# Ternary weights prepared in 42 pieces, one order of halves in the fp4 stages, memories prepared in the first attention

## The chip, the cores and the metric

The kernel runs on one core of one Trainium2 chip. The metric is device time in microseconds (us); lower is better. It runs one fixed program over a batch of 8 sequences of 1024 tokens with 256 features, in float32.

## The reference, cut to what matters

Six sublayers follow each other, each on a layer norm of x:

```python
x = x + 0.5 * fp4_ffn(layernorm(x))        # blockwise FP4 rounding of inputs, weights and hidden values
x = x + decay_attention(layernorm(x))      # a decaying state per head
x = x + 0.5 * fp4_ffn(layernorm(x))
x = x + 0.5 * ternary_ffn(layernorm(x))    # W1, W2 rounded to -1, 0, 1; gelu between them
x = x + memory_attention(layernorm(x))     # linear attention beside 4 stored memories
x = x + 0.5 * ternary_ffn(layernorm(x))
```

The ternary rounding takes one scale for a whole matrix, so nothing can be rounded before everything has been summed:

```python
scale = max(mean(abs(w)), 1e-8)
w_t = clip(round(w / scale), -1, 1)
```

The FP4 rounding scales each block of 16 values by its largest magnitude and rounds to eight magnitudes.

## The kernel before, in words

The 8192 tokens are 64 tiles of 128 rows; four tiles are a group (G = 4), so there are 16 groups. x stays in SBUF through all six stages. The stages run one after the other: `ffn_fp4`, `attn_decay`, `ffn_fp4`, `ffn_ternary`, `attn_memory`, `ffn_ternary`.

The order of instructions on each engine is written out by hand: `pin` ties an instruction behind the last pinned one on its engine, so each engine works its list strictly in order. A late instruction therefore holds everything behind it on the same engine.

**An fp4 stage** is a loop over iterations i, one tile each (i is its number, j = i % 4 its place in the group). In iteration i:
- PE multiplies x of the tile with gate and up weights (pg, pu at L835), turns the scales of tile i-1 (pts, L863), and multiplies tile i-4 with the down weights (po, L932).
- ACT does silu (sg, L846), copies scales (L790), takes magnitudes of tile i-1 (qp, L795) and copies the turned scales (sct, L869).
- VectorE (DVE) forms h = sg * pu (L848), rounds h of tile i-1 to the grid in two steps (L858), finds the scales of h (L783 to L787), and adds po to x at the end of the iteration (L941).
- POOL multiplies h by the inverse scales (h, L791) and the turned grid by its scales (ht, L899), which for tile i-3 comes in iteration i.
- SP issues the DMAs: scales out (sd, L871), the transpose of the grid (gt, L884), the spread scales back (L876).

**The coming group's input** goes the same way, half a group (two tiles, 512 columns) at a time: normalise on ACT (xn, L317 and L325, four instructions a half), scale on DVE (xn, L783) and POOL (xn, L791), magnitudes on ACT (mgx) and grid on DVE (L858), transpose by DMA (gtx, L1048), multiply on POOL (xt, L899). xn is one buffer. For group t the first half is normalised in iteration 4t-7 and the second in 4t-5 (odd iterations), scaled in 4t-6 and 4t-4, rounded in 4t-5 and 4t-3. The transposed grid lies in xn itself, so a half of xn is written again only when its transpose has been read.

**Layer norm statistics** are planned ahead: `statistics(sizes, dues)` spreads the shares (one per tile, four sets of terms per batch of groups; L235 to L264) evenly over the iterations before each batch is due. `PLANS` holds the sizes and due iterations. What is due at 0 is done in the last iterations of the stage before (`begin`).

**Side work of the first fp4 stage** hangs at the end of each iteration, in `prepared(i)`, behind that iteration's L941:
- the FP4 rounding of the down weights (iterations 1 to 5),
- the decay tables for the attention (`prep_decay`, POOL, iterations 7, 11, 15, 19),
- the ternary weights. Each matrix is 2048 columns of 128 partitions. Its load is issued in iteration 7 (w1) and 27 (w2); then come, in every fourth iteration, the sums (one reduction over 2048, L683), the total (a matmul and two small instructions), and two halves of rounding of 1024 columns, each of three DVE instructions (L699, L700, L703). That is 4 pieces a matrix, in iterations 11, 15, 19, 23 and 31, 35, 39, 43.
- in iteration 44 `prep_memory`: one DMA (b2h), 16 POOL and 3 DVE instructions (L720 to L741) that make tables for the later stages.

**The first attention** (`attn_decay`) is a loop over the same 64 tiles; DVE weighs scores (L1259), POOL only adds a bias to x once a group.

Of the kernel before, what the change touches and what calls it, by code (L numbers as in the profile page):

```python
# [18 lines left out]
P = 128  # L19
# [20 lines left out]
def macaron_kernel(  # L40
# [227 lines left out]
    def statistics(sizes, dues):  # L268
# [75 lines left out]

    NT = NG * G
    PLANS = {
        "start": ((2, 1, 1, 2, 4, 4, 2), [max(0, G * (g - 2) + 1) for g in range(NG)]),
        "fp4": ((2, 1, 1, 2, 4, 4, 2), [max(0, G * (g - 2) + 1) for g in range(NG)]),

        "decay": ((2, 2, 4, 4, 4), [max(0, G * g - 5) for g in range(NG)]),  # L350
        "ternary": ((2, 2, 4, 4, 4), [max(0, g - 1) for g in range(NG)]),
# [321 lines left out]

    def prep_ternary(w, raw_w, prep, ps, tag):

        n0 = w.shape[1]
        n = n0 * w.shape[2]
        ab = prep.tile([P, 1], F32, tag="t_ab", name="t_ab")
        rc = prep.tile([P, 1], F32, tag="t_rc", name="t_rc")

        def sums():
            pin(
                nc.vector.tensor_reduce(  # L683
                    ab, raw_w.rearrange("p k n -> p (k n)"), AX.X, ALU.add,
                    apply_absolute_value=True,
                )
            )

        def total():
            pa = ps.tile([P, 1], F32, tag=tag, name="pa")  # L690
            pin(nc.tensor.matmul(pa, lhsT=ones, rhs=ab, start=True, stop=True))
            pin(nc.vector.tensor_scalar(rc, pa, 1.0 / (P * n), 1e-8, ALU.mult, ALU.max))
            pin(nc.vector.reciprocal(rc, rc))

        def rounded(q):
            part = slice(q * n0 // 2, (q + 1) * n0 // 2)
            wf = raw_w[:, part, :].rearrange("p k n -> p (k n)")
            lo = prep.tile([P, n // 2], F32, tag="t_lo", name="t_lo")
            pin(nc.vector.tensor_scalar(wf, wf, rc, None, ALU.mult))  # L699
            pin(nc.vector.tensor_scalar(lo, wf, -0.5, None, ALU.is_lt))  # L700

            pin(
                nc.vector.scalar_tensor_tensor(  # L703
                    w[:, part, :].rearrange("p k n -> p (k n)"), wf, 0.5, lo,
                    ALU.is_gt, ALU.subtract,
                )
            )

        return sums, total, lambda: rounded(0), lambda: rounded(1)

    memb = w_l1.tile([P, 2, NM, 2, HD], F32, name="memb")

# [32 lines left out]
    def ffn_fp4(prepare, after):  # L745
        with ExitStack() as st:
# [150 lines left out]
            def multiplied(wide, grid):  # L897
                pin(
                    nc.gpsimd.tensor_tensor(  # L899
                        wide.rearrange("p c t -> p (c t)"), grid.rearrange("p c t -> p (c t)"),  # L900
                        wide.rearrange("p c t -> p (c t)"), ALU.mult,
                    )
                )
# [42 lines left out]
            def prepared(i):  # L946

                if i in (1, 3):
                    prep_down_scale(i // 2)
                elif i in (2, 4):  # L950
                    prep_down(i // 2 - 1)
                if i == DOWN:
                    raw_stack.close()
                    load_a0()
                if i % G == 3 and i < 5 * G and i > G:
                    prep_decay(i // G - 1)
                for k, i0 in enumerate((7, 27)):
# [27 lines left out]
            sc1 = fp4_scale(v1, lnp, nc.gpsimd, pin)  # L985
            xts[1] = (xn1,)

            xn = None
            downs = 0

            def x_part(half):
                return xn[:, 2 * half : 2 * half + 2, :].rearrange("p t d -> p (t d)")

            for i in range(NT + 3):
                g, j = divmod(i, G)
                h = hp.tile([P, NI], F32, tag="h", name="h") if i < NT else None

                to = (i + 7) // G
                to_do = to < NG and i > 0
                half = 0 if j in (1, 2, 3) else 1  # L1000
                if i == 0 and not prepare:
                    xts[0], copied = turn_products(xts[0])
                    copied()
# [37 lines left out]
                        round_(part, sc, mg, nc.vector if q else nc.gpsimd)  # L1041
                if pts is not None:
                    spread(i - 1, pts)
                for to_, half_ in list(xgrids):
# [5 lines left out]
                if i == 0:  # L1050
                    mgs = [qp[:, 0 : 2 * D], ps_t.tile([P, 2 * D], F32, tag="pt", name="mg1")]
                    for n in range(2):
# [1 line left out]
                if 0 < i < NT:  # L1054

                    ln.advance(i - 1, 1)
                if to_do and j % 2 == 1:
                    if j == 1:
                        to_n, tiles = to, (0, 1)
                        if xn is None:  # L1060
                            xn = xn_pool.tile([P, G, D], F32, tag="xn", name="xn")
                    else:
                        to_n, tiles = (i + 5) // G, (2, 3)
                    if to_n < NG:
                        for n in tiles:
                            ln.normalize(xn, to_n, n, pin)
                if by_dma(i - 3):
                    scaled_turn(i - 3)
                if NT - 2 <= i - 2 < NT:
                    turn(i - 2)  # L1070
                for key in list(xgrids):
                    gt, at = xgrids[key]
                    if at == i - 2:
                        xgrids.pop(key)
                        to_m, half_m = key
                        multiplied(xts[to_m][:, G * half_m : G * half_m + G, :], gt)
                if i < NT:
                    own = scales[i % 2] if by_dma(i) else None
                    if own is not None:
                        scale(h, hp, NI, sc=own[:, : NI // 16])  # L1080
                        hs[i] = (h, own)
                    else:
                        hs[i] = (h, scale(h, hp, NI) if i < NT - 1 else None)

                    if j % 2 == 0 and i > 1:
                        to_s, half_s = ((i + 6) // G, 0) if j == 2 else ((i + 4) // G, 1)
                        if 1 < to_s < NG:
                            scale(
                                x_part(half_s), lnp, NI + 88,
                                sc=own[:, NC * 8 : NC * 8 + 2 * D // 16],  # L1090
                            )
                            xhalf[i] = (to_s, half_s)
                    if j % 2 == 1 and i > 1:
                        to_r, half_r = ((i + 5) // G, 0) if j == 3 else ((i + 3) // G, 1)
                        if 1 < to_r < NG:
                            v = x_part(half_r)
                            mg = ps_t.tile([P, 2 * D], F32, tag="pt", name="mgx")
                            magnitudes(v, mg)
                            gx = v.bitcast(BF16)[:, 0 : 2 * D]
                            round_grid(v, mg, gx)  # L1100
                            xgrids[to_r, half_r] = (gx, i)
# [252 lines left out]
    def attn_decay(after):  # L1354
        with ExitStack() as st:
# [101 lines left out]
            for i in range(n + 3):  # L1457
# [627 lines left out]
```

## Time and profile before

| | us |
|---|---|
| median of 3 runs | 2608.78 (2608.46 to 2609.09) |
| profiled execution | 2604.35 |
| its span (first to last instruction) | 2602.6 |
| PE busy | 2504.2 (96%) |
| DVE busy | 2107.9 (81%) |
| ACT busy | 1235.8 (47%) |
| POOL busy | 902.6 (35%) |

The stages, by the lines that stand in the trace: the first fp4 stage begins its tiles at 37 us and ends near 540, the first attention runs to about 1000, the second fp4 stage to about 1490, and the two ternary stages with the second attention between them fill the rest.

How to read it: "busy" is time in which an engine executed instructions, registers and waits not counted. Idle time of an engine that is not the bottleneck costs nothing, so a share over the whole span says little about one stage. Where a stage is measured in what follows, it is cut out of the span in us from the first instruction. A tile of an fp4 stage is counted from the first sg<-pg (L846) of one tile to that of the next. DVE and POOL durations are those of single instructions; a duration longer than the instruction's usual one means that it was held while it ran.

### The profile page before, as it was taken

To read this page: it belongs to the slowest core of one execution; us is meant where nothing else is said; L and a number is where in the kernel's file an instruction comes from. 1 tells how busy PE (TensorE), PEld (TensorE's weight loads), DVE (VectorE), ACT (ScalarE), POOL (GpSimd) and SP (SyncE) were. 2 spreads that over 40 slices of the span, in tenths; PEclk is the share of its full clock that TensorE was granted. 3 is DMA by queue.
4 is the path that set the end of the run, shared out by engine and by line. 5 is a ranking of instruction groups with operands and counts; after the bars stand their busy time and mean duration, and the time that the engine had idled before them with its cause. 6 is when DMAs were issued, how large, how long until landed. Compare 5 with 4: busy or idle time off the path is not lost.

```text
span 2602.6 us, 52695 instructions
## 1 busy us (share of the span) xinstructions
PE 2504.2 (96%) x20426; PEld 1864.2 (72%) x20426; DVE 2107.9 (81%) x5040; ACT 1235.8 (47%) x2785; POOL 902.6 (35%) x895
## 2 busy tenths in 40 slices
PE   4899999999999998999999999999999999999999
PEld 2566776766666665677777789995677767678998
DVE  7899999858777678998889789657888888879864
ACT  5344444433433333444444366665555555437664
POOL 4555555521100102555555400004555555540000
PEclk9899999999999999999999999999999999999999
DMA  7455565510000001556555300000000000000001
GB/s 218 99 111 120 119 114 112 110 32 2 2 2 2 2 2 29 113 117 116 115 114 118 81 1 1 1 1 1 2 2 2 2 2 2 2 2 25 33 33 42
DMA packets 197883, 130.32 MB, mean 50 GB/s; under 512 B 137824, under 2 KB 173696, under 8 KB 197632
## 3 DMA queue, kind: packets, MB, share of 16 engines
q1 hardware_dynamic: 196688, 125.75, 22.3%
q8 instruction: 161, 2.64, 0.4%
q0 software_dynamic: 240, 0.54, 0.1%
q14 instruction: 90, 0.74, 0.1%
q10 hardware_dynamic: 704, 0.66, 0.1%
HBM read 78.67 MB, written 16.52 MB: 37 GB/s over the span
## 4 chain that ended last, share of the span: by engine, by line
PE 80%; DVE 11%; ACT 3%; DMA 3%; issue 2%; POOL 1%; SPq 1%; DVEq 0%; POOLq 0%; ACTq 0%
PE po L932 10%; PE po L1207 9%; PE pg L835 9%; PE ph L1180 9%; PE pu L835 8%; PE sc L1250 5%; PE py L1334 5%; PE pq L1348 4%; PE pkv L1348 4%; PE pk L1348 4%; PE po L1348 4%; PE py L1316 2%; PE pmo L1765 2%; DVE at L1259 1%; DMA gtx<-xn 1%
## 5 line engine op out<-in xcount | busy, mean ns | idle before, releaser
L835 PE MATMUL pg<-wgu,xt 128*128 128x352 f32 x1024 | 350.0, 465 | 13.4 <-ACT sg L846 13.1
L932 PE MATMUL po<-wd,ht 128*128 128x256 f32 x1536 | 356.0, 382 | 2.3 <-DVE x L941 1.8
L835 PE MATMUL pu<-wgu,xt 128*128 128x352 f32 x1024 | 348.9, 464 | 2.1 <-DVE h L848 1.9
L932 PEld LDWEIGHTS po<-wd,ht 128*128 128x128 f32 x1536 | 291.7, 191 | 66.0 <-issue 4.1
L791 POOL TENSOR_TENSOR h<-h,q_rs 128x704 f32<-128x704 f32 (+1 forms) x128 | 176.3, 1378 | 419.9 <-DVE q_rs L787 419.9
L846 ACT ACTIVATE sg<-pg 128x352 f32<-128x352 f32 x256 | 117.8, 460 | 399.3 <-PE pg L835 394.0
L835 PEld LDWEIGHTS pg<-wgu,xt 128*128 128x128 f32 x1024 | 194.9, 192 | 108.5 <-ACT sg L846 21.1
L835 PEld LDWEIGHTS pu<-wgu,xt 128*128 128x128 f32 x1024 | 187.1, 193 | 103.3 <-issue 14.7
L1207 PE MATMUL po<-w,hl 128*128 128x256 f32 x1024 | 243.9, 280 | 1.4 <-DVE hl L1191 1.2
L1207 PE MATMUL po<-w,hh 128*128 128x256 f32 x1024 | 243.4, 280 | 0.0
L1881 POOL TENSOR_TENSOR mo<-mo 128x256 f32<-128x256 f32 x192 | 164.3, 856 | 195.0 <-DVE mo L1778 186.5
L899 POOL TENSOR_TENSOR ht<-gt,ht 128x768 f32<-128x768 bf16 x124 | 206.4, 1664 | 0.0
L1180 PE MATMUL ph<-xh,w 128*128 128x512 f32 x512 | 204.4, 401 | 1.4 <-ACT hf L1188 0.6
L1180 PE MATMUL ph<-xl,w 128*128 128x512 f32 x512 | 202.2, 396 | 0.0
L1191 DVE TENSOR_TENSOR hl<-hf,hh 128x512 fp32r<-128x512 f32 x256 | 168.2, 683 | 39.6 <-ACT hh L1189 36.1
L1207 PEld LDWEIGHTS po<-w,hl 128*128 128x128 f32 x1024 | 192.1, 188 | 4.5 <-DVE hl L1191 2.5
L1207 PEld LDWEIGHTS po<-w,hh 128*128 128x128 f32 x1024 | 192.0, 188 | 2.6 <-DVE x L1215 0.3
L848 DVE TENSOR_TENSOR h<-sg,pu 128x352 f32<-128x352 f32 x256 | 131.6, 514 | 60.0 <-PE pu L835 53.1
L1188 ACT ACTIVATE hf<-ph,b1c 128x512 f32<-128x512 f32 x256 | 168.3, 696 | 18.5 <-PE ph L1180 16.1
L1259 DVE TENSOR_TENSOR at<-sc,dec 128x512 f32<-128x512 f32 x256 | 158.5, 681 | 16.6 <-PE sc L1250 16.5
L1259 DVE TENSOR_TENSOR at<-sc,tri 128x512 f32<-128x512 f32 x256 | 164.6, 678 | 0.4 <-PE sc L1250 0.4
L1189 ACT CAST hh<-hf 128x512 fp32r<-128x512 f32 x256 | 149.2, 628 | 17.0 <-PE po L1207 15.2
(276 smaller groups left out, 5304.0 us busy)
## 6 DMA issues: line engine op xcount, KB each, us to landing
ht<-sd SPq DMA_DIRECT2D x124, 384.0 KB
xt<-sd SPq DMA_DIRECT2D x56, 256.0 KB
sd<-sct SPq DMA_DIRECT2D x124, 64.0 KB
x<-in_x SPq DMA_DIRECT2D x15, 512.0 KB
out<-x SPq DMA_DIRECT2D x15, 512.0 KB
raw_w<-in_w_t SPq DMA_DIRECT2D x2, 1024.0 KB
gt<-gd SPq DMA_TRANSPOSE x124
gtx<-xn SPq DMA_TRANSPOSE x56
```

The source lines that it names most:

```text
L791: pin(mul.tensor_tensor(vb, vb, rs[:, :, None].to_broadcast([P, nb, 16]), ALU.mult))
L835: nc.tensor.matmul(ps, lhsT=xts[g][:, 2 * j + k, :], rhs=wgu[:, k, (2 * q + of_up) * NHALF : (2 * q + of_up + 1) * NHALF], start=(k == 0), ...
L899: nc.gpsimd.tensor_tensor(wide.rearrange("p c t -> p (c t)"), grid.rearrange("p c t -> p (c t)"), wide.rearrange("p c t -> p (c t)"), ALU. ...
L932: nc.tensor.matmul(po, lhsT=ht[:kn, c, :], rhs=wd[:kn, c, :], start=(c == 0), stop=(c == NC - 1),)
L1180: nc.tensor.matmul(ph, lhsT=w1[:, k, f * P : (f + 1) * P], rhs=xt[:, k, :], start=(k == 0 and xt is xh), stop=(k == 1 and xt is xl),)
L1188: nc.scalar.activation(hf, ph, AF.Gelu, bias=b1c[:, f : f + 1])
L1189: nc.scalar.copy(hh[:, f, :], hf)
L1191: nc.vector.tensor_tensor(hl[:, f, :], hf, hh[:, f, :].bitcast(F32), ALU.subtract)
L1207: nc.tensor.matmul(po, lhsT=ht[:, f, j * P : (j + 1) * P], rhs=w2[:, f, :], start=(f == 0 and ht is hh), stop=(f == NF - 1 and ht is hl),)
L1259: nc.vector.tensor_tensor(at, sc.rearrange("p m (e t) -> p (m e) t", e=2), weight, ALU.mult)
L1348: nc.tensor.matmul(dst, lhsT=lhsT, rhs=rhs, start=n == 0, stop=n == len(parts) - 1)
L1881: summed = nc.gpsimd.tensor_tensor(mo[:, :, :, 0, :], mo[:, :, :, 0, :], mo[:, :, :, m, :], ALU.add)
```

## The change

- `PLANS`: in the stage that follows the start, each batch of statistics is due one iteration later (4g-6 in place of 4g-7); in "fp4" (the second fp4 stage) the first batch has three groups in place of two, all done ahead of the stage.
- Halves: for every group from the third on both halves follow one table. The first half is normalised and scaled in iteration 4t-6 and rounded in 4t-5; the second in 4t-4 and 4t-3. Scaling and rounding stay in their iterations; normalising moves one iteration later, into the one that scales. The gtx transpose and POOL's xt multiplication swap places in the text of an iteration.
- Ternary weights: the sums come in four parts of 512 columns, the rounding in 16 parts of 128, one piece in every iteration: 21 pieces a matrix, 42 in all. w1: sums in iterations 9 to 12, total in 13, rounding in 14 to 29. w2 is loaded in 34: sums in 36 to 39, total in 40, rounding in 41 to 56. The three instructions of a rounding piece are the same as before.
- `prep_memory` moves from iteration 44 of the first fp4 stage to iteration 24 of the first attention.

```diff
-        "start": ((2, 1, 1, 2, 4, 4, 2), [max(0, G * (g - 2) + 1) for g in range(NG)]),
-        "fp4": ((2, 1, 1, 2, 4, 4, 2), [max(0, G * (g - 2) + 1) for g in range(NG)]),
+        "start": (
+            (2, 1, 1, 2, 4, 4, 2), [0 if g < 2 else G * (g - 2) + 2 for g in range(NG)]
+        ),
+        "fp4": ((3, 1, 2, 4, 4, 2), [0 if g < 3 else G * (g - 2) + 2 for g in range(NG)]),
...
-        def sums():
+        n_sums, n_parts = 4, 16
+        def sums(q):
+            part = slice(q * n // n_sums, (q + 1) * n // n_sums)
...
         def total():
-            pa = ps.tile([P, 1], F32, tag=tag, name="pa")
+            pa = ps.tile([P, n_sums], F32, tag=tag, name="pa")
             pin(nc.tensor.matmul(pa, lhsT=ones, rhs=ab, start=True, stop=True))
-            pin(nc.vector.tensor_scalar(rc, pa, 1.0 / (P * n), 1e-8, ALU.mult, ALU.max))
+            pin(nc.vector.tensor_reduce(rc, pa, AX.X, ALU.add))
+            pin(nc.vector.tensor_scalar(rc, rc, 1.0 / (P * n), 1e-8, ALU.mult, ALU.max))
             pin(nc.vector.reciprocal(rc, rc))
         def rounded(q):
-            part = slice(q * n0 // 2, (q + 1) * n0 // 2)
-            lo = prep.tile([P, n // 2], F32, tag="t_lo", name="t_lo")
+            part = slice(q * n // n_parts, (q + 1) * n // n_parts)
+            lo = prep.tile([P, n // n_parts], F32, tag="t_lo", name="t_lo")
             pin(nc.vector.tensor_scalar(wf, wf, rc, None, ALU.mult))
             pin(nc.vector.tensor_scalar(lo, wf, -0.5, None, ALU.is_lt))
...
-                for k, i0 in enumerate((7, 27)):
+                for k, i0 in enumerate((7, 34)):
...
-                    if i0 < i <= i0 + 16 and i % G == i0 % G:
-                        raw_w[1][(i - i0) // G - 1]()
-                    if i == i0 + 16:
+                    if i0 + 1 < i <= i0 + 1 + 21:
+                        raw_w[1][i - i0 - 2]()
+                    if i == i0 + 22:
                         raw_w_stack.close()
-                if i == 44:
-                    with behind():
-                        prep_memory()
...
+            norms, x_scales, x_rounds = {}, {}, {}
+            for t in range(2, NG):
+                for half in range(2):
+                    at = G * t - 6 + 2 * half
+                    norms[at] = x_scales[at] = x_rounds[at + 1] = (t, half)
...
-                if to_do and j % 2 == 1:
-                    if j == 1:
-                        to_n, tiles = to, (0, 1)
...
+                if i in norms:
+                    if xn is None:
+                        xn = xn_pool.tile([P, G, D], F32, tag="xn", name="xn")
+                    t, half = norms[i]
+                    for n in (2 * half, 2 * half + 1):
+                        ln.normalize(xn, t, n, pin)
...
+                if i == 24:
+                    with behind():
+                        prep_memory()
```

More of the change, by code (lines that the diff above doesn't have):

```diff
@@ L674, in prep_ternary @@
     def prep_ternary(w, raw_w, prep, ps, tag):
-        n0 = w.shape[1]
-        n = n0 * w.shape[2]
-        ab = prep.tile([P, 1], F32, tag="t_ab", name="t_ab")
+        wv = w.rearrange("p k n -> p (k n)")
+        rv = raw_w.rearrange("p k n -> p (k n)")
+        n = rv.shape[1]
+        n_sums, n_parts = 4, 16
+        ab = prep.tile([P, n_sums], F32, tag="t_ab", name="t_ab")
         rc = prep.tile([P, 1], F32, tag="t_rc", name="t_rc")
-        def sums():
+        def sums(q):
+            part = slice(q * n // n_sums, (q + 1) * n // n_sums)
             pin(
                 nc.vector.tensor_reduce(
-                    ab, raw_w.rearrange("p k n -> p (k n)"), AX.X, ALU.add,
-                    apply_absolute_value=True,
+                    ab[:, q : q + 1], rv[:, part], AX.X, ALU.add, apply_absolute_value=True
                 )
@@ L689, in total @@
         def total():
-            pa = ps.tile([P, 1], F32, tag=tag, name="pa")
+            pa = ps.tile([P, n_sums], F32, tag=tag, name="pa")
             pin(nc.tensor.matmul(pa, lhsT=ones, rhs=ab, start=True, stop=True))
-            pin(nc.vector.tensor_scalar(rc, pa, 1.0 / (P * n), 1e-8, ALU.mult, ALU.max))
+            pin(nc.vector.tensor_reduce(rc, pa, AX.X, ALU.add))
+            pin(nc.vector.tensor_scalar(rc, rc, 1.0 / (P * n), 1e-8, ALU.mult, ALU.max))
             pin(nc.vector.reciprocal(rc, rc))
         def rounded(q):
-            part = slice(q * n0 // 2, (q + 1) * n0 // 2)
-            wf = raw_w[:, part, :].rearrange("p k n -> p (k n)")
-            lo = prep.tile([P, n // 2], F32, tag="t_lo", name="t_lo")
+            part = slice(q * n // n_parts, (q + 1) * n // n_parts)
+            wf = rv[:, part]
+            lo = prep.tile([P, n // n_parts], F32, tag="t_lo", name="t_lo")
             pin(nc.vector.tensor_scalar(wf, wf, rc, None, ALU.mult))
@@ L703, in rounded @@
                 nc.vector.scalar_tensor_tensor(
-                    w[:, part, :].rearrange("p k n -> p (k n)"), wf, 0.5, lo,
-                    ALU.is_gt, ALU.subtract,
-                )
-            )
-        return sums, total, lambda: rounded(0), lambda: rounded(1)
+                    wv[:, part], wf, 0.5, lo, ALU.is_gt, ALU.subtract
+                )
+            )
+        return (
+            [lambda q=q: sums(q) for q in range(n_sums)] + [total]
+            + [lambda q=q: rounded(q) for q in range(n_parts)]
+        )
     memb = w_l1.tile([P, 2, NM, 2, HD], F32, name="memb")
@@ L996, in ffn_fp4 @@
                 h = hp.tile([P, NI], F32, tag="h", name="h") if i < NT else None
-                to = (i + 7) // G
-                to_do = to < NG and i > 0
-                half = 0 if j in (1, 2, 3) else 1
                 if i == 0 and not prepare:
@@ L1043, in ffn_fp4 @@
                     spread(i - 1, pts)
+                if i == 0:
+                    mgs = [qp[:, 0 : 2 * D], ps_t.tile([P, 2 * D], F32, tag="pt", name="mg1")]
+                    for n in range(2):
+                        magnitudes(v1[:, 2 * D * n : 2 * D * (n + 1)], mgs[n])
+                if 0 < i < NT:
+                    ln.advance(i - 1, 1)
+                if by_dma(i - 3):
+                    scaled_turn(i - 3)
+                for key in list(xgrids):
+                    gt, at = xgrids[key]
+                    if at == i - 2:
+                        xgrids.pop(key)
+                        to_m, half_m = key
+                        multiplied(xts[to_m][:, G * half_m : G * half_m + G, :], gt)
                 for to_, half_ in list(xgrids):
@@ L1049, in ffn_fp4 @@
                         xgrids[to_, half_] = (gt, at)
-                if i == 0:
-                    mgs = [qp[:, 0 : 2 * D], ps_t.tile([P, 2 * D], F32, tag="pt", name="mg1")]
-                    for n in range(2):
-                        magnitudes(v1[:, 2 * D * n : 2 * D * (n + 1)], mgs[n])
-                if 0 < i < NT:
-                    ln.advance(i - 1, 1)
-                if to_do and j % 2 == 1:
-                    if j == 1:
-                        to_n, tiles = to, (0, 1)
[L1060 to L1068, printed above, removed]
+                if i in norms:
[4 more added lines that the diff above has]
+                        ln.normalize(xn, t, n, pin)
                 if NT - 2 <= i - 2 < NT:
                     turn(i - 2)
[L1071 to L1076, printed above, removed]
                 if i < NT:
@@ L1083, in ffn_fp4 @@
                         hs[i] = (h, scale(h, hp, NI) if i < NT - 1 else None)
[L1085 to L1101, printed above, removed]
+                    if i in x_scales:
+                        scale(
+                            x_part(x_scales[i][1]), lnp, NI + 88,
+                            sc=own[:, NC * 8 : NC * 8 + 2 * D // 16],
+                        )
+                        xhalf[i] = x_scales[i]
+                    if i in x_rounds:
+                        v = x_part(x_rounds[i][1])
+                        mg = ps_t.tile([P, 2 * D], F32, tag="pt", name="mgx")
+                        magnitudes(v, mg)
+                        gx = v.bitcast(BF16)[:, 0 : 2 * D]
+                        round_grid(v, mg, gx)
+                        xgrids[x_rounds[i]] = (gx, i)
                     if i == 0:
```

## The prediction

> **What bounds the kernel now.** I read the page's part 1, then the chain of waits, then stretches cut tile by tile, then both engines' timelines where VectorE (DVE) and GpSimd (POOL) meet. Part 1: TensorE is busy nearly always.
>
> ```profile
> PE 2504.2 (96%) x20426; PEld 1864.2 (72%) x20426; DVE 2107.9 (81%) x5040; ACT 1235.8 (47%) x2785; POOL 902.6 (35%) x895
> ```
>
> In the first fp4 stage the chain of waits shows undisturbed tiles like this (start us, us, what):
>
> ```profile
> 302.35 1.18 PE pg L835 x4
> 303.53 1.18 PE pu L835 x4
> 304.71 1.18 PE pg L835 x4
> 306.00 1.19 PE pu L835 x4
> 307.19 2.59 PE po L932 x12
> 309.78 1.18 PE pg L835 x4
> ```
>
> From pg to pg is 309.78 - 302.35 = 7.43 us: a tile's floor. The starts of the first sg<-pg of each tile give tiles 6 to 62 of stage 1 as 101.1 to 538.9: 437.8 us for 57 tiles, 14.3 over 57 x 7.43 = 423.5. That is all a better first fp4 stage can win there. Stage 2 from tile 5 (1046.1 to 1480.5, 58 tiles) is 3.5 over.
>
> The table of stretches has tiles 14 to 29 and 41 to 56 of stage 1, then the same tiles of stage 2, which has no ternary work (us, PE, PEld, DVE, ACT, POOL busy, clock, DMA share, GB/s):
>
> ```profile
> 165.10:288.70 123.60, 120.55 (x467) 85.75 (x466) 114.55 (x256) 50.92 (x129) 69.97 (x57) 1.00 0.60 120
> 371.00:493.70 122.70, 119.81 (x465) 85.64 (x464) 111.53 (x246) 50.88 (x128) 70.59 (x65) 1.00 0.57 116
> 1116.00:1235.20 119.20, 119.20 (x465) 86.05 (x465) 109.19 (x250) 50.93 (x129) 67.00 (x49) 1.00 0.60 117
> 1317.00:1435.90 118.90, 118.90 (x465) 86.11 (x464) 104.82 (x233) 51.03 (x128) 65.75 (x49) 1.00 0.57 115
> ```
>
> Without ternary work PE is never idle, but DVE is busy 109.2 and 104.8 of 119, before its gaps of 0.034 us between dependent instructions: about 0.3 to 0.6 us a tile is free. The change puts 16 pieces into each of the first two stretches.
>
> **What a piece meets.** Wherever a TENSOR_SCALAR that reads and writes SBUF alone (L671, L699, L700, L255, L721, L737) starts on DVE under a running POOL instruction, the timelines read alike: it ends only after that POOL instruction has ended. DVE, then POOL:
>
> ```profile
> 118.39 1.46 DVE L671 TENSOR_SCALAR bqp<-bq,pm 128x2 f32<-128x2 f32 x2
> ...
> 364.28 1.64 DVE L699 TENSOR_SCALAR raw_w<-raw_w,t_rc 128x1024 f32<-128x1024 f32 x1
> 365.96 0.69 DVE L700 TENSOR_SCALAR t_lo<-raw_w 128x1024 f32<-128x1024 f32 x1
> 366.68 1.23 DVE L703 SCALAR_TENSOR_TENSOR w<-raw_w,t_lo 128x1024 fp32r<-128x1024 f32 x1
> ```
>
> ```profile
> 118.05 1.65 POOL L899 TENSOR_TENSOR ht<-gt,ht 128x768 f32<-128x768 bf16 x1
> ...
> 363.72 1.65 POOL L899 TENSOR_TENSOR ht<-gt,ht 128x768 f32<-128x768 bf16 x1
> ```
>
> Two elements (L671) took 1.33 us and ended at 119.72, 0.02 after POOL's ht (118.05 + 1.65 = 119.70). L699 ran 0.54 us after ht's end (363.72 + 1.65 = 365.37 to 365.92). So the wait is set by the POOL instruction, not by the piece's size. At 212.92 L700 took 2.03 instead of 0.69: ht had queued behind L699 and went in between. The sums (L683, one input) took 2.28 beside an ht, no more than when POOL was idle.
>
> Where POOL stands when a piece comes, from POOL's timeline (start, us; bracket: idle before):
>
> ```profile
> 165.46 1.39 POOL L791 TENSOR_TENSOR h<-h,q_rs 128x704 f32<-128x704 f32 x1 [2.09 <-DVE q_rs L787]
> 166.80 1.66 POOL L899 TENSOR_TENSOR ht<-gt,ht 128x768 f32<-128x768 bf16 x1
> 172.56 1.39 POOL L791 TENSOR_TENSOR h<-h,q_rs 128x704 f32<-128x704 f32 x1 [4.10 <-DVE q_rs L787]
> 173.97 1.06 POOL L791 TENSOR_TENSOR xn<-xn,q_rs 128x512 f32<-128x512 f32 x1
> 174.98 1.65 POOL L899 TENSOR_TENSOR ht<-gt,ht 128x768 f32<-128x768 bf16 x1
> ```
>
> Let R be the end of h's reciprocal (L787) on DVE, 165.31 in the odd iteration and 172.42 in the even one. POOL starts h 0.14 later, so ht ends at R + 3.15 in odd iterations and, behind xn, at R + 4.21 in even ones; these offsets repeat in nearly every tile. DVE's last work of an iteration is L941 (x<-po); with one statistics share it ends at R + 2.1. The piece stands right behind L941 in every iteration, so it meets xn or ht each time.
>
> **The pieces.** Own time: L255 takes 0.164 us for 16 elements and L700 0.694 for 1024, so 128 take about 0.22; L703 (1.23 for 1024) and L264 (0.17 for 16) give 0.29. A piece is 0.22 + 0.22 + 0.29 and two gaps of 0.034, 0.80 us. Blocked, the first instruction ends 0.06 after ht, then 0.25 and 0.32: R + 4.84 even, R + 3.79 odd. From there to the next R is the fixed front (gated, two rounding steps, gated, scale): 172.42 - 167.88 = 4.54, less 0.09 overlap. A pair takes 4.84 + 3.79 + 9.08 - 0.18 = 17.53 us of DVE, against 2 x 7.43 = 14.87 on PE. DVE then sets the pace, PE waits in h<-sg,pu.
> - w1: 8 x 17.53 = 140.2, plus one set of terms on DVE (0.41 at 185.0, 1.91 at 191.8): 142.5 against 123.6 now: **+18.9**.
> - w2: 142.5 against 122.7: **+19.8**. This stretch holds the memories' preparation now (tiles 45 to 47: 8.31, 9.68, 7.80), so its going is in the 122.7.
> - In even iterations POOL's xt (1.17 us) starts at R + 4.4 to 4.9, when the piece's third instruction asks (R + 4.55). No L703 met POOL; the nearest row is a DVE TENSOR_TENSOR of two SBUF inputs at L802, 1.91 us long, which ended 0.37 after POOL's ht. Bounds 0 and 16 x 1.17 = 18.7; I take a third, **+6**, as most xt come later than R + 4.55.
> - Sums: four of about 0.6 (L783: 0.64 for 512) for one of 2.28, and one more small reduce: +0.6 a weight, where w1's lie among full tiles and w2's in free ones. The later starts (34 for 27) move it, no more. I take 0 against the lost mgx waits below.
>
> [...]
>
> **The order of halves.** Four ACT instructions of 0.5 us a half move one iteration later, out of the odd iteration, where ACT xn L317 waited for the transpose gtx (36.1 us in 23 waits in stage 1) and held mgx, for which DVE waited 5.9 us (12 times; 3.0 in stage 2). In the even iteration they stand behind sct; there sct ends at 1193.55, four of them would end at 1195.6, and DVE reads xn at 1196.61: 1 us to spare, cost 0; 2.0 us a pair if that cover went. POOL's xt still waits for the same transpose. The gain is DVE time outside the blocked stretches: -1 in stage 1, -1 in stage 2 (bounds 0 and 9). On SP and POOL the order of instructions stays, but for w2's load and b2h.
>
> **Statistics.** In stage 2 group 2's 3.82 us of statistics in tile 1 (12.16 long, DVE busy 11.37) go to the end of the first attention (16 shares for 12 in 12 iterations; DVE 47 of 65 us there). I take -3 (0 to -4). In stage 1 they spread over two iterations that DVE fills anyway: 0.
>
> **The memories' preparation** is 16 POOL instructions (4.3 us), three on DVE (0.73, 1.04, 0.16, most of it blocked) and one DMA, for which DVE waited 1.92. In attention POOL is busy 7 of 65 us; b2h's load is issued earlier on SP, ahead of the last spreads, so DVE finds it there; behind the three stand x<-po and the at products, with 18 us idle in 65. Cost 0; some 0.7 if DVE were full.
>
> **Sum:** 18.9 + 19.8 + 6 - 1 - 1 - 3 = +39.7. On the profiled execution's 2604.35 us (span 2602.6) that is 2644.0; the median of the runs, 2608.78, lies 4.4 above, so **2648.5 us**.
>
> **Rivals.**
> - *POOL does not hold the pieces* (they fall into its gaps). A pair needs 13.07 + 1.6 = 14.67, about 15.1 with shares and terms: -1.9 and -2.7, with the other gains -9.6: 2599, faster. It decides below about 0.35 us of blocking a piece; I count 1.1 odd and 2.1 even, and the rows above speak against it. Chance 6%, one of it within 0.2%.
> - *PE bounds every tile*: 14.3 + 5 saved, 2590. It needs 0.8 us free a tile, and there is 0.6. Chance 3%.
> - *Half the blocking*, pieces arriving late into ht as at 395.55 (L699 0.78): 51/2 less, 2612 to 2636. Chance 13%.
> - *The third instruction blocked too*, every time, and more POOL work in line: 2664 to 2685. Chance 13%.
> - My forecast, 2636 to 2664: 65%.
>
> A measurement tells about 0.2% from no change. Faster 8%, within 3%, slower 89%. The range runs from half blocking to the full price of xt and a little more: 2618 to 2672.
>
> **What would show it.** In the new trace: tiles 14 to 29 and 41 to 56 of stage 1 near 8.8 to 9.3 us a tile with PE idle about a sixth; the first instruction of even pieces 1.5 to 2.3 us long, ending with POOL's ht; mgx waits gone; tile 1 of stage 2 near 9 us; attention unchanged. Pieces of 0.2 us each beside a busy POOL, or 7.43 us tiles, would prove me wrong.

## The result, and the profile after

The changed kernel takes 2638.98 us (median of 4 runs, 2637.34 to 2639.66) beside 2608.62 of the kernel before (4 runs, 2607.13 to 2609.09): a ratio of 1.0116, 95% interval 1.0099 to 1.0134. It is 30.4 us slower; 39.7 us slower had been forecast. Its profiled execution took 2638.43 us.

The page's first part and the shares of its chain of waits, of the changed kernel; the last line is the chain of the kernel before:

```profile
PE 2514.7 (95%) x20426; PEld 1867.4 (71%) x20426; DVE 2155.6 (82%) x5120; ACT 1231.3 (47%) x2785; POOL 900.8 (34%) x895
```

```profile
PE 74%; DVE 18%; issue 3%; ACT 2%; POOL 1%; DMA 0%; ACTq 0%; DVEq 0%; POOLq 0%; SPq 0%
```

```profile
PE 80%; DVE 11%; ACT 3%; DMA 3%; issue 2%; POOL 1%; SPq 1%; DVEq 0%; POOLq 0%; ACTq 0%
```

DVE is busy 47.7 us more (2155.6 - 2107.9), though the two matrices hold no more numbers. TensorE does the same work (20426 matmuls in both, busy 2504.2 us before and 2514.7 after). Where DVE carries the chain is seen in a stretch of it in the first stage (start us, us, what):

```profile
250.41 1.20 PE pg L842 x4
...
251.63 0.52 DVE h L855
...
256.15 1.10 DVE raw_w L704
...
257.27 0.24 DVE t_lo L705
...
257.75 0.51 DVE h L855
258.26 0.81 DVE h L865
...
259.90 0.52 DVE h L855
```

Ahead of the change an undisturbed tile ran on PE from pg to pg in 7.43 us. Here the chain leaves PE at 251.6 and stays on DVE, through the piece (L704, L705), until 263.3. The stretches of the 16 tiles that follow the pieces of w1 and of w2 (us, PE, PEld, DVE, ACT, POOL busy, clock, DMA share, GB/s):

```profile
169.50:312.90 143.40, 124.99 (x465) 85.22 (x464) 137.48 (x294) 50.57 (x128) 69.13 (x56) 0.99 0.48 98
395.70:536.90 141.20, 124.25 (x465) 85.97 (x464) 135.58 (x279) 50.60 (x129) 64.43 (x48) 0.99 0.47 95
```

PE is idle 18.4 and 17.0 us, DVE busy 137.5 of 143.4. The same cut for the kernels of this study, from the first sg<-pg of a tile to that of another (a piece in iteration i delays the next tile, so tiles 15 to 30 and 42 to 57 are counted):

| us | tiles 0-5 | 6-14 | 15-30 (w1) | 31-41 | 42-57 (w2) | 58-61 | first attention | stage 2, 0-5 | stage 2, 6-61 | rest |
|---|---|---|---|---|---|---|---|---|---|---|
| before | 63.6 | 71.4 | 123.6 | 83.3 | 121.7 | 30.3 | 476.1 | 47.6 | 418.0 | 1129.5 |
| after | 61.1 | 71.4 | 143.4 | 82.7 | 141.2 | 31.3 | 476.0 | 40.9 | 418.2 | 1133.4 |
| e1 pieces alone | 64.7 | 71.3 | 142.6 | 84.5 | 140.9 | 31.5 | 475.8 | 47.1 | 418.1 | 1134.3 |
| e2 no pieces | 62.1 | 71.9 | 122.7 | 82.7 | 119.9 | 30.5 | 474.4 | 40.9 | 418.4 | 1133.5 |
| e3 through PSUM | 61.1 | 71.5 | 139.6 | 82.0 | 134.2 | 30.3 | 474.4 | 40.9 | 417.7 | 1129.8 |
| e4 memories alone | 63.5 | 71.4 | 124.3 | 83.5 | 119.5 | 29.9 | 474.4 | 47.6 | 418.0 | 1129.7 |
| e5 own PSUM tile | 61.0 | 71.5 | 124.9 | 83.6 | 121.3 | 30.0 | 474.6 | 42.6 | 418.1 | 1129.2 |
| e6 pairs, POOL idle | 62.1 | 71.7 | 124.3 | 82.0 | 121.3 | 29.8 | 476.0 | 40.9 | 418.0 | 1132.4 |
| e7 halves alone | 61.6 | 70.6 | 120.9 | 82.7 | 122.1 | 30.2 | 474.4 | 45.1 | 418.1 | 1133.3 |
| e8 eight pieces | 61.3 | 69.7 | 119.4 | 81.8 | 119.7 | 29.7 | 474.4 | 40.9 | 417.7 | 1132.8 |
| e9 three groups ahead | 64.3 | 71.4 | 125.0 | 83.4 | 122.6 | 30.4 | 475.9 | 42.5 | 418.0 | 1130.8 |

The rest of the span and the attention move by up to 5 us from execution to execution in no order that fits an edit; so single spans are not compared below, only stages, and medians of runs. From before to after the two rounding stretches cost +19.8 and +19.5; tiles 0 to 5 give -2.5, stage 2 -6.5, the others +0.3. With the stage's own start (-0.4) that is 30.2, and the medians say 30.4. The rest of the span is left out of this sum; it is 3.9 longer in this one execution (1133.4 and 1129.5), so the two profiled spans differ by 34.1.

Inside a pair of tiles, DVE and then POOL of the changed kernel:

```profile
247.06 0.56 DVE L704 TENSOR_SCALAR raw_w<-raw_w,t_rc 128x128 f32<-128x128 f32 x1
247.65 1.58 DVE L705 TENSOR_SCALAR t_lo<-raw_w 128x128 f32<-128x128 f32 x1
249.26 0.29 DVE L708 SCALAR_TENSOR_TENSOR w<-raw_w,t_lo 128x128 fp32r<-128x128 f32 x1
...
256.06 1.18 DVE L704 TENSOR_SCALAR raw_w<-raw_w,t_rc 128x128 f32<-128x128 f32 x1
257.27 0.23 DVE L705 TENSOR_SCALAR t_lo<-raw_w 128x128 f32<-128x128 f32 x1
257.54 0.29 DVE L708 SCALAR_TENSOR_TENSOR w<-raw_w,t_lo 128x128 fp32r<-128x128 f32 x1
```

```profile
246.47 1.06 POOL L798 TENSOR_TENSOR xn<-xn,q_rs 128x512 f32<-128x512 f32 x1
247.49 1.66 POOL L906 TENSOR_TENSOR ht<-gt,ht 128x768 f32<-128x768 bf16 x1
249.30 1.28 POOL L906 TENSOR_TENSOR xt<-gtx,xt 128x512 f32<-128x512 bf16 x1 [0.16 <-DMA gtx<-xn]
...
255.50 1.65 POOL L906 TENSOR_TENSOR ht<-gt,ht 128x768 f32<-128x768 bf16 x1
```

In the even iteration L704 starts under xn and ends at 247.61, 0.08 after xn (246.47 + 1.06 = 247.53). ht has stood behind xn and starts at 247.49, before L705 can; L705 then takes 1.58 instead of 0.23 and ends 0.08 after ht. So one piece is held twice; 14 of the 16 even pieces went this way. In the odd iteration ht alone holds L704, to 257.24 (ht ends 257.15).

The third instruction met POOL as well, where xt had started before it. DVE, then POOL:

```profile
174.55 0.23 DVE L705 TENSOR_SCALAR t_lo<-raw_w 128x128 f32<-128x128 f32 x1
174.81 1.21 DVE L708 SCALAR_TENSOR_TENSOR w<-raw_w,t_lo 128x128 fp32r<-128x128 f32 x1
```

```profile
174.71 1.17 POOL L906 TENSOR_TENSOR xt<-gtx,xt 128x512 f32<-128x512 bf16 x1 [0.27 <-DMA gtx<-xn]
```

xt began 0.10 ahead of L708, and L708 took 1.21 where 0.29 is usual. At 249.26, above, L708 began 0.04 ahead of xt and took 0.29. L708 was held by xt in 5 of the 16 even pieces (1.13 to 1.21 each).

### The profile page after: what moved, and what is told of

It is laid out like the page before. It is cut to its first block, busy times and chain, and to the rows that moved or that the text cites. A ratio compares the mean times of both kernels' runs of the same rounds, so it can differ in the third digit from the quotient of the medians.

```text
span 2636.7 us, 52777 instructions
## 1 busy us (share of the span) xinstructions
PE 2514.7 (95%) x20426; PEld 1867.4 (71%) x20426; DVE 2155.6 (82%) x5120; ACT 1231.3 (47%) x2785; POOL 900.8 (34%) x895
## 4 chain that ended last, share of the span: by engine, by line
PE 74%; DVE 18%; issue 3%; ACT 2%; POOL 1%; DMA 0%; ACTq 0%; DVEq 0%; POOLq 0%; SPq 0%
PE po L1204 9%; PE po L939 9%; PE ph L1177 8%; PE pg L842 6%; PE pu L842 6%; PE sc L1247 5%; PE py L1331 4%; PE pq L1345 4%; PE pkv L1345 4%; PE pk L1345 4%; PE po L1345 4%; DVE qp L790 3%; PE py L1313 2%; DVE h L855 2%; PE pmo L1765 2%
## 5 line engine op out<-in xcount | busy, mean ns | idle before, releaser
L939 PE MATMUL po<-wd,ht 128*128 128x256 f32 x1536 | 361.7, 386 | 15.2 <-DVE x L948 13.9
L842 PEld LDWEIGHTS pg<-wgu,xt 128*128 128x128 f32 x1024 | 194.4, 191 | 106.3 <-ACT sg L853 19.8
L1185 ACT ACTIVATE hf<-ph,b1c 128x512 f32<-128x512 f32 x256 | 167.7, 695 | 17.7 <-PE ph L1177 16.1
```

The costliest lines, as they stand in the source:

```text
L842: nc.tensor.matmul(ps, lhsT=xts[g][:, 2 * j + k, :], rhs=wgu[:, k, (2 * q + of_up) * NHALF : (2 * q + of_up + 1) * NHALF], start=(k == 0), ...
L939: nc.tensor.matmul(po, lhsT=ht[:kn, c, :], rhs=wd[:kn, c, :], start=(c == 0), stop=(c == NC - 1),)
L1185: nc.scalar.activation(hf, ph, AF.Gelu, bias=b1c[:, f : f + 1])
```

## The experiments

The theory: a rounding piece costs what it does because its first two instructions read and write SBUF alone and are held until POOL's running multiplication ends. The rival: the count of small instructions is what costs, wherever they stand. For the smaller parts: which of them gives what.

### e1: the pieces alone

The kernel before, with the ternary part of the change and nothing else:

```diff
+        n_sums, n_parts = 4, 16
...
-                for k, i0 in enumerate((7, 27)):
+                for k, i0 in enumerate((7, 34)):
...
+                    if i0 + 1 < i <= i0 + 1 + 21:
+                        raw_w[1][i - i0 - 2]()
```

> The kernel before with the 42 ternary pieces alone (old order of halves, old plans, memories still prepared in iteration 44). Theory (POOL's ht and xt hold each piece until they end): the two stretches of 16 tiles cost 19.8 and 19.6 us as in the change, and the memories' preparation, which the change takes out of the second stretch, stays in it for about 3 more: 2608.6 + 42 = 2651 us (2645 to 2656). Rival (a piece costs only its own 0.80 us, and the rest of the loss comes from the order of halves): 25.6 us of own time against 15 us of free DVE and 7 us of old pieces in full tiles: about +5, 2614 us.

Measured: 2646.93 us (2644.09 to 2649.81) beside 2608.51; ratio 1.0149 (1.0134 to 1.0164). The pieces alone lose 38.4 us; the other parts of the change give some back.

### e2: all but the pieces

The changed kernel with the four large pieces of before:

```diff
-        n_sums, n_parts = 4, 16
...
+            part = slice(q * n0 // 2, (q + 1) * n0 // 2)
...
-                for k, i0 in enumerate((7, 34)):
+                for k, i0 in enumerate((7, 27)):
```

> The changed kernel with the ternary weights prepared in the old 4 pieces a matrix, in the old iterations: order of halves, plans and memories as changed. Theory: what is left of the change gains: 3 us at the start of stage 1, 6.4 us in stage 2, about 3 us for the memories and 1 us of mgx waits: 2608.6 - 13 = 2595 us (2592 to 2600). Rival (the order of halves loses): above 2608.

Measured: 2594.44 us (2592.70 to 2596.53) beside 2608.51; ratio 0.9948 (0.9933 to 0.9963). Without the pieces the change is a gain of 14.1 us; with them it loses 30.4.

### e3: the product in PSUM, in a tile that ACT uses too

The changed kernel with the product of weight and scale written to columns 864 to 992 of the PSUM tile qp, and the other two instructions reading it there:

```diff
-            pin(nc.vector.tensor_scalar(wf, wf, rc, None, ALU.mult))
-            pin(nc.vector.tensor_scalar(lo, wf, -0.5, None, ALU.is_lt))
+            pin(nc.vector.tensor_scalar(scr, wf, rc, None, ALU.mult))
+            pin(nc.vector.tensor_scalar(lo, scr, -0.5, None, ALU.is_lt))
...
+                            w, raw_w[0], pool, ps_t, "pt", qp[:, 864:992]
```

> The changed kernel with the same 42 pieces in the same places, but the product w / scale is put into 128 free columns of a PSUM tile, so that each of the three instructions reads or writes at most one SBUF tensor on its input side beside PSUM. Theory (only the holding by POOL costs): pieces of about 1.0 us unheld, a pair 15.6 us for 17.9, so 16 x 2.3 = 37 us less than the changed kernel: 2602 us (2597 to 2609). Rival (number and fixed cost of the instructions): not less than the changed kernel, 2639 to 2645 us.

Measured: 2625.77 us (2619.17 to 2627.79) beside 2608.51; ratio 1.007 (1.0053 to 1.0087). A miss by 24 us. DVE's timeline of e3, then ACT's:

```profile
258.71 0.34 DVE L704 TENSOR_SCALAR qp<-raw_w,t_rc 128x128 f32<-128x128 f32 x1
259.09 0.29 DVE L705 TENSOR_SCALAR t_lo<-qp 128x128 f32<-128x128 f32 x1
259.41 0.29 DVE L708 SCALAR_TENSOR_TENSOR w<-qp,t_lo 128x128 fp32r<-128x128 f32 x1
...
260.91 0.89 DVE L865 SCALAR_TENSOR_TENSOR h<-qp,h 128x704 f32<-128x704 f32 x1 [0.77 <-ACT qp L802]
```

```profile
259.74 0.28 ACT L797 COPY sc<-qp 128x44 f32<-128x44 f32 x2 [2.32 <-DVE w L708]
260.11 0.76 ACT L802 ACTIVATE qp<-h 128x704 f32<-128x704 f32 x1
```

The holds are gone: 0.34, 0.29, 0.29. A wait stands in their place: ACT's copy out of the tile qp is released by the piece's last instruction (its end, 259.70; the copy at 259.74), the magnitudes (L802) queue behind it, and DVE waits 0.77 for them. Over the kernel DVE's wait for qp is 30.0 us in 44 waits, against 7.3 in 15 after the change; the 22.7 more are nearly the whole miss. So this run tells of the shared tile, not of the count of instructions; e5 was made to tell them apart.

### e5: the product in a PSUM tile of its own

```diff
-            pin(nc.vector.tensor_scalar(wf, wf, rc, None, ALU.mult))
-            pin(nc.vector.tensor_scalar(lo, wf, -0.5, None, ALU.is_lt))
+            scr = ps.tile([P, n // n_parts], F32, tag=tag, name="scr")
+            pin(nc.vector.tensor_scalar(scr, wf, rc, None, ALU.mult))
+            pin(nc.vector.tensor_scalar(lo, scr, -0.5, None, ALU.is_lt))
...
-                    wv[:, part], wf, 0.5, lo, ALU.is_gt, ALU.subtract
+                    wv[:, part], scr, 0.5, lo, ALU.is_gt, ALU.subtract
```

> The changed kernel with the product weight times scale of each rounding piece put into a PSUM tile of its own instead of back into SBUF; number, order and place of the pieces are unchanged. In e3 the product shared a PSUM tile with ACT's magnitudes, which made DVE wait for ACT about 0.7 us a tile. Theory (the cost of the pieces is that a TENSOR_SCALAR from SBUF to SBUF is held by POOL's running multiplication): without the hold and without the shared tile a pair of tiles costs about 7.43 x 2 plus at most 0.6, so 2602 (2596 to 2612). Rival (the number of small instructions is what costs, 0.9 us a tile whatever they read and write): 2626 or more.

Measured: 2599.2 us (2593.7 to 2600.39) beside 2606.53; ratio 0.9964 (0.995 to 0.9978). The same 42 pieces in the same places, with the same number of instructions, are now about 38 us cheaper: 7.3 below the kernel before of this series of runs, where the changed kernel stood 30.4 above that of its own. DVE of e5, then POOL:

```profile
249.59 0.35 DVE L705 TENSOR_SCALAR scr<-raw_w,t_rc 128x128 f32<-128x128 f32 x1
249.97 0.29 DVE L706 TENSOR_SCALAR t_lo<-scr 128x128 f32<-128x128 f32 x1
250.29 0.29 DVE L709 SCALAR_TENSOR_TENSOR w<-scr,t_lo 128x128 fp32r<-128x128 f32 x1
```

```profile
249.00 1.06 POOL L799 TENSOR_TENSOR xn<-xn,q_rs 128x512 f32<-128x512 f32 x1
250.02 1.65 POOL L907 TENSOR_TENSOR ht<-gt,ht 128x768 f32<-128x768 bf16 x1
```

POOL is busy through the whole piece, and no instruction of it is held; over all 32 pieces L705 took 0.337 to 0.347. The third now has one input in PSUM and passes beside ht in 0.29.

### e6: the same pieces where POOL is idle

The changed kernel, SBUF to SBUF, two pieces at a time ahead of the scale of h in even iterations:

```diff
+            def early(i):
+                for i0 in (7, 34):
+                    n = i - i0 - 7
+                    if 0 <= n < 16 + i % 2 and (i % 2 == 0):
+                        k = n // 2 * 2
+                        raw_w[1][5 + k]()
+                        raw_w[1][5 + k + 1]()
...
-                    if i0 + 1 < i <= i0 + 1 + 21:
+                    if i0 + 1 < i <= i0 + 1 + 5:
...
+                if prepare:
+                    early(i)
```

> The changed kernel with the same 32 rounding pieces of 128 columns, SBUF to SBUF, the same instructions and the same number, but two pieces at a time in every even iteration, ahead of the first instruction of that iteration's scale of h, where POOL has finished ht of the iteration before and waits for the next h. Theory (the hold by POOL is the cost): a pair of tiles falls from 17.4 to about 15.3 us, 16 pairs less 2.1 us are 34 less: 2602 (2595 to 2608). Rival (the count of small instructions is the cost): 2639, no change from the changed kernel.

Measured: 2596.75 us (2595.95 to 2597.43) beside 2606.53; ratio 0.9959 (0.9945 to 0.9972). Moved by a few instructions, the pieces are about 40 us cheaper (9.8 below the kernel before, where the changed kernel stood 30.4 above). The rival falls twice, here and in e5. DVE of e6, then POOL, whose bracket gives its idle time before:

```profile
261.23 0.28 DVE L704 TENSOR_SCALAR raw_w<-raw_w,t_rc 128x128 f32<-128x128 f32 x1
261.55 0.23 DVE L705 TENSOR_SCALAR t_lo<-raw_w 128x128 f32<-128x128 f32 x1
261.81 0.29 DVE L708 SCALAR_TENSOR_TENSOR w<-raw_w,t_lo 128x128 fp32r<-128x128 f32 x1
```

```profile
264.78 1.39 POOL L798 TENSOR_TENSOR h<-h,q_rs 128x704 f32<-128x704 f32 x1 [5.57 <-DVE q_rs L794]
```

The price of the hold in one table: the groups of DVE by line and shape, all 32 pieces (busy us, mean ns | idle before). The changed kernel:

```profile
L704 DVE TENSOR_SCALAR raw_w<-raw_w,t_rc 128x128 f32<-128x128 f32 x32 | 29.5, 922 | 0.0
L705 DVE TENSOR_SCALAR t_lo<-raw_w 128x128 f32<-128x128 f32 x32 | 26.3, 823 | 1.1
L708 DVE SCALAR_TENSOR_TENSOR w<-raw_w,t_lo 128x128 fp32r<-128x128 f32 x32 | 13.9, 433 | 1.1
```

And e6:

```profile
L708 DVE SCALAR_TENSOR_TENSOR w<-raw_w,t_lo 128x128 fp32r<-128x128 f32 x32 | 9.4, 292 | 1.1
L704 DVE TENSOR_SCALAR raw_w<-raw_w,t_rc 128x128 f32<-128x128 f32 x32 | 8.9, 279 | 0.0
L705 DVE TENSOR_SCALAR t_lo<-raw_w 128x128 f32<-128x128 f32 x32 | 7.3, 227 | 1.1
```

69.7 us with POOL in the way, 25.6 without: 44.1 us of hold on an engine that sets the pace.

### e4: the memories alone

The kernel before, with the memories' preparation moved:

```diff
-                if i == 44:
-                    with behind():
-                        prep_memory()
...
+                if i == 24:
+                    with behind():
+                        prep_memory()
```

> The kernel before with the memories' preparation alone moved into the first attention. Theory: tiles 45 to 47 of stage 1 lose their excess of about 3 us and the attention takes it for nothing: 2605.5 us (2604 to 2607). Rival (it is paid in the attention): 2608 to 2610.

Measured: 2605.62 us (10 runs, 2602.24 to 2610.19) beside 2608.51 (13 runs); ratio 0.9991 (0.9982 to 1.0). A gain of about 2.9, whose interval touches no gain; in the table tiles 42 to 57 fall from 121.7 to 119.5 and the attention pays nothing that shows.

### e7: the order of halves alone

The kernel before, with the new table of halves, and with the transpose and POOL's multiplication swapped as in the change; plans, ternary work and memories as they were:

```diff
+            norms, x_scales, x_rounds = {}, {}, {}
+            for t in range(2, NG):
+                for half in range(2):
+                    at = G * t - 6 + 2 * half
+                    norms[at] = x_scales[at] = x_rounds[at + 1] = (t, half)
```

> The kernel before with the one order of halves alone: normalising one iteration later, the transpose and POOL's multiplication swapped; old statistics plans, old four-piece ternary work, memories in iteration 44 of the first stage. The changed kernel without its pieces was 14.1 below the kernel before, of which moving the memories gave 2.9. Theory (the statistics plans carry most of the other 11, as the tiles 0 to 5 of both fp4 stages show 3.0 and 5.1 less): 2606 (2604 to 2608.5), at most 3 less than before. Rival (the order of halves carries it): 2597 to 2601.

Measured: 2598.3 us (2596.6 to 2598.67) beside 2606.53; ratio 0.9962 (0.9948 to 0.9976). A miss: 8.2 us where at most 3 were expected, inside the rival's range. What went is ACT's wait for the transpose, from 36.1 us in 23 waits in the first stage before to one in the same stage of e7 (a line of ACT's waits, us 99 to 536: in total, times, longest):

```profile
ACT xn L317 <- DMA gtx<-xn: 3.1, 1, 3.1
```

With it DVE's waits for mgx are gone: 5.9 us in the first stage, 9.1 us in 21 waits over both fp4 stages before, none in e7. Whether the later normalising or the swap removed them was not tried. Tiles 15 to 30 fall from 123.6 to 120.9, tiles 0 to 5 from 63.6 to 61.6, and in stage 2 from 47.6 to 45.1.

### e9: three groups ahead of the second fp4 stage

```diff
-        "fp4": ((2, 1, 1, 2, 4, 4, 2), [max(0, G * (g - 2) + 1) for g in range(NG)]),
+        "fp4": ((3, 1, 2, 4, 4, 2), [0 if g < 3 else G * (g - 2) + 1 for g in range(NG)]),
```

> The kernel before with one part of the statistics plans alone: the second fp4 stage's first batch holds three groups in place of two, all done in the last iterations of the first attention; everything else, the order of halves too, as before. Theory (the attention has room on DVE for 16 shares in place of 12, and the 3.8 us of group 2 leave tile 1 of the stage, where PE stood idle): 3 to 4.5 less than before, so 2602 to 2604 beside 2606.5, with tile 1 of the second fp4 stage near 6 us in place of 12.2 and the attention unchanged at 474 to 476. Rival (the shares delay the attention's end as much as they free the stage): 2606, no change.

Measured: 2601.03 us (11 runs, 2598.99 to 2604.11) beside 2606.95 (15 runs); ratio 0.9977 (0.9968 to 0.9986). 5.9 less, a little more than the 3 to 4.5 expected, and 5.1 of it are in the trace where they were expected: tile 1 of stage 2 takes 6.04 us, was 12.16; tiles 0 to 5 take 42.5, were 47.6; the attention 475.9, was 476.1. The rival falls: the attention had room.

### e8: a version that beats both

The changed kernel with 8 pieces of 256 columns a matrix in place of 16, one in each even iteration ahead of the scale of h, loads in iterations 15 and 37:

```diff
-        n_sums, n_parts = 4, 16
+        n_sums, n_parts = 4, 8
...
+            def early(i):
+                for i0 in (15, 37):
+                    n = i - i0 - 7
+                    if 0 <= n < 16 and i % 2 == 0:
+                        raw_w[1][5 + n // 2]()
...
-                for k, i0 in enumerate((7, 34)):
+                for k, i0 in enumerate((15, 37)):
...
-                    if i0 + 1 < i <= i0 + 1 + 21:
+                    if i0 + 1 < i <= i0 + 1 + 5:
...
+                if prepare:
+                    early(i)
```

> The changed kernel with its rounding in 8 pieces of 256 columns a matrix in place of 16 of 128, each in an even iteration ahead of that iteration's scale of h, where POOL is idle; loads in iterations 15 and 37, sums in one iteration each after it. Theory (hold by POOL is the cost, DVE's own time of a piece, about 0.34 + 0.34 + 0.45 us, fits in the slack of a pair of tiles): 2590 (2587 to 2595), below the 2594.4 of the changed kernel with the old four large pieces. Rival (small slack: DVE sets the pace by 0.5 us or more a pair): 2596 to 2602.

Measured: 2588.88 us (2585.1 to 2592.58) beside 2606.53; ratio 0.9927 (0.9914 to 0.994). The two stretches of e8, columns as above:

```profile
167.00:286.40 119.40, 119.38 (x467) 86.17 (x466) 113.99 (x270) 50.48 (x129) 69.27 (x57) 1.00 0.59 117
371.00:490.00 119.00, 118.72 (x464) 85.77 (x463) 111.06 (x262) 50.17 (x128) 65.23 (x49) 1.00 0.59 115
```

PE is no longer idle beside the ternary work. The first of these stretches holds w1's sums and the first half of its pieces, which run from 224.8 to 329; over 223 to 345 PE is idle 0.02 us of 122. A whole 256-column piece takes 0.35 + 0.29 + 0.43 us; 16 of them are 17.0 us of DVE against 25.6 for 32 of half the size. So the cutting alone was not the fault; the place behind L948 was, and the pieces were smaller than they had to be. That eight pieces beat the four large ones of e2 is not shown: e8 is 17.7 below the kernel before of its series, e2 14.1, and the intervals of the two ratios overlap.

## Why the prediction was right, and where its sizes were off

- **What bounds the kernel, and what a piece meets: right.** DVE became the pace of both stretches (busy 137.5 of 143.4 us and 135.6 of 141.2), held by POOL (44.1 us over the 32 pieces). e5 takes the hold away by where the product goes, e6 by when the piece comes, and they give back about 38 and 40 us. PE was idle about an eighth of the stretches, not a sixth.
- **The pieces (18.9 + 19.8, and 6 for the third instruction: 44.7) measured 39.3.** Own times were right but for one: L704 takes 0.28 unheld, not 0.22; L705 0.23 and L708 0.29. That makes 0.80 without the gaps (e6). The odd tile was forecast at 8.24 us and took 8.27. The even one was forecast at 9.29 and took 9.09: the prediction let the first instruction be held until ht's end and the other two follow it. In the trace xn holds the first and ht the second, so only the third is left when ht ends. So the sign that the prediction named, a first instruction of 1.5 to 2.3 us that ends with ht, came in one of the 16 even pieces (1.63). Over 16 pairs by 0.17 that is an estimated 2.7 us. The 6 for the third instruction was the author's estimate, which no row of the kernel before shows: there no L703 met POOL. In the changed kernel xt held it in 5 even pieces of 16, not in a third of xt's full price each time: 4.3 us for the 6. Some 1.0 us are not assigned; in iteration 19 the piece ran among POOL's short decay steps and took 0.39, 0.38 and 0.45.
- **The sums (0).** They are four of 0.675 us a weight for one of 2.28. The prediction's remark that a sum beside ht takes no more than with POOL idle has no row for the idle case: POOL was working when both sums of the kernel before began, at 150.86 and 304.12. It was busy for 2.24 us of the first sum's 2.276 and for 1.62 of the second's 2.275.
- **The order of halves (-1 and -1, bounds 0 and 9): too small.** Alone it gives 8.2 (e7). The prediction read 5.9 and 3.0 us of waits for mgx and took 2 of them, on the ground that only DVE time outside the blocked stretches counts; e7, which has no blocked stretches, wins 8.2 where 9.1 us of such waits went. That they are the source of the whole 8.2 is argued from the size, not shown. In the changed kernel only part of it comes through. Tiles 0 to 5 of stage 1 take 61.0 to 62.1 us in every kernel with the new order and 63.5 to 64.7 in every one with the old, about -2.5. In stage 2 it seems to add 1.6 to what e9 gives (42.5 to 40.9), but e5, which has both, took 42.6, so one execution of each does not settle it. In the rounding stretches it gives nothing: e1 has 142.6 and 140.9, the changed kernel 143.4 and 141.2.
- **Statistics (-3 in stage 2, 0 to -4; 0 in stage 1): too small.** e9 shows -5.1 in tiles 0 to 5 of stage 2. The prediction priced the 3.82 us of DVE work that leave tile 1; PE's idle time there fell from 5.71 to 0.62. Tile 1 was forecast near 9 us and took 5.66. What the later due times in stage 1 do by themselves was not tried.
- **The memories: right.** Costs 0 in the attention; e4's 2.9 had been put into the 122.7 that the second stretch was counted from.
- **The sum.** 5.4 of the 9.5 us between 2648.5 and 2638.98 are the rounding, about 4.1 the gains of the other parts (-9.1 in the table's stages, -5 forecast). Both errors point the same way; neither hides the other.
- **The rivals.** POOL not holding the pieces (2599) describes e5 (2599.2), the kernel in which that condition is made true. PE bounding every tile (2590) describes e8 (2588.88). Neither condition held in the changed kernel. That the times agree so closely is luck: against the kernel before of its own series e5 is 7.3 lower where the rival said 9.6, and e8 17.7 where the other said 19.3.

Apart, the memories give 2.9, the halves 8.2 and the plan of stage 2 5.9, 17.0 in all; together 14.1 (e2). The difference is within what these intervals allow. Some of it may be overlap in tiles 0 to 5 of stage 2 (2.5 + 5.1 apart; together 6.7, but 5.0 in e5).

## What to carry to other kernels

Before work is cut into pieces to fill an engine's gaps, look at what the neighbour engine runs in those gaps: here L704, which takes 0.28 us unheld, took 0.56 under what was left of xn (at 247.06) and 1.18 under what was left of ht (at 256.06), and a smaller one paid no less: two columns in the kernel before (L671) took 1.33 under ht. The 32 pieces together paid 44.1 us of hold. Where POOL was idle, or with the product in a PSUM tile of their own, the same pieces cost 4 to 7 us more than the four large ones of e2, not 44 (each run taken against the kernel before of its series). When an edit has several parts, run it without the costly one: 14 us of gain were hidden under 44 of loss.

## What the hardware showed that was not expected

- In 14 of the 16 even pieces a POOL instruction that stood behind another (ht behind xn) began before the piece's second instruction could (247.49 and 247.65), so that a piece of 0.8 us was held by two POOL instructions one after the other: at 247.06 L704 took 0.56 us under xn, then L705 1.58 under ht.
- The SCALAR_TENSOR_TENSOR of two SBUF inputs (L708) was held as well (1.13 to 1.21 us under xt, 0.45 once under a decay step, 0.29 otherwise) where POOL's instruction had started first, by as little as 0.10 us; started 0.04 us ahead of xt it took 0.29.
- Unrelated columns of one PSUM tile tied two engines together in e3: ACT's copy waited for DVE's piece (it started at 259.74, 0.04 after the piece's end), and DVE then 0.77 and 0.69 us for ACT (at 260.91 and 269.71; over the kernel 30.0 us in 44 waits, against 7.3 in 15 after the change). The traces show the releaser; whether it is the program's own bookkeeping of the tile or the chip was not tried.
- TENSOR_SCALAR with a scale for each partition from SBUF (L704) takes 0.279 us for 128 columns and 0.346 for 256; the one with a constant (L705) 0.227 and 0.294. Twice the columns cost 0.067 more in each.
